# An earlier load of the next batch, and the last batch's masks, sums and row blocks placed otherwise, in a two-layer graph kernel

## The chip, the cores and the metric

The kernel runs on one core of one Trainium2 chip. The metric is the device time of the program in microseconds; three runs of the kernel before gave 4035.16, 4039.82 and 4045.39 us, the median is 4039.82 us. The profile that is quoted was taken from an execution of its own, with a span of 4048.5 us from the first to the last instruction.

Names in the profile: PE is TensorE's matmul, PEld its weight load, DVE is VectorE, ACT is ScalarE, POOL is GpSimd, SP is SyncE, whose queue (SPq) issues the transfers. L390 is line 390 of the kernel.

## The reference

Thirty-two independent batches `x[b]` of 512 nodes by 512 features go through two layers on one graph `adj` (512x512, zeros and ones), all in float32:

```python
# layer 0
deg = a.sum(axis=1)
out = deg[None, :, None] * (x @ Wi.T + b0) + einsum('ij,bjo->bio', a, x @ Wj.T)
x = layernorm(x + out)
# layer 1: attention with 8 heads of 64, masked by the graph
q, k, v = split_heads(x @ Wq.T + bq), split_heads(x @ Wk.T + bk), split_heads(x @ Wv.T + bv)
scores = where(adj == 0, -inf, q @ k.T / 8)
x = layernorm(x + (softmax(scores) @ v).reshape(...) @ Wo.T + bo)
```

## The kernel before

The program is one long sequence without a loop, with a schedule written by hand. Three batches are in work at once: while batch `b = n - 1` is in its attention (one "period" of eight steps), the products of batch `n` (layer 0, then Q, K, V), the start of batch `n + 1` and the output product of batch `n - 2` are placed between the steps as "pieces". A piece is a part of a 512x512x512 product by a seven-product scheme, with weights from a ring of twelve tiles that the sync queue fills. `z(...)` marks work that TensorE does not do.

Three buffers `xh` hold x, which is also where the result grows. So the load of batch `n + 1` needs the buffer whose last use is the store of batch `n - 2`:

```python
def load_x(b):
    XT[b] = work([P, NC, D], "xh", 3)
    nc.sync.dma_start(XT[b], rows(x[b]))
def store(b):
    nc.sync.dma_start(rows(out[b]), XT.pop(b))

def split(b, dc):            # x in two parts, for a product by adjR in a faster format
    ...
    nc.scalar.copy(hi, xs)                      # L183
    nc.gpsimd.tensor_sub(lo, xs, hi.bitcast(FT))  # L184
def ahead(b):
    split(b, 0)
    split(b, 1)

def l0_gather(b, dc, bank, adjT=None):
    ...
    for jc in range(NC):
        nc.tensor.transpose(pt[...], xt[:, jc, ...], ident)   # L292
    nc.vector.tensor_mul(XD[b][:, dc, :], pt, deg_r)          # L293
    ...
    nc.tensor.matmul(pm, parts[w][:, jc, :], adjR[:, jc, :], ...)  # L299, hi then lo
    nc.scalar.copy(AX_T[b][:, dc, :], pm)                     # L305
```

The part of a period in which Q, K and V are made, `ORDER` being `(1, 2, 6, 7, 4, 5, 3)`:

```python
    if m >= 0:
        res += [z(apply, m, 0), z(apply, m, 1), z(store, m)]
    for i in ORDER[2:]:
        for f in pc("q", n, i, K), pc("v", n, i, A):
            res += [f] + [g for g in side[:1] if g]
            side = side[1:]
        if i == 5 and n + 1 < B:
            res += [z(load_x, n + 1)] if n > 0 else []
    if n + 1 < B:
        res += [z(ahead, n + 1)]
    return res
```

Behind it comes `phase_a(n + 1)`, which begins with the four gathers of batch `n + 1`.

A step of the attention takes half the keys of a pair of heads. Blocks `kc` 0 and 1 belong to `half` 0, blocks 2 and 3 to `half` 1:

```python
def scores(b, hp, kc):
    ps = sc_tile()                                  # in PSUM, two of them
    for s in range(2): nc.tensor.matmul(ps[:, s, :], KT..., QT...)            # L427
    e = E[kc] = work([P, 2, N], "e", 4)
    nc.scalar.activation(ps, ps, AF.Exp, scale=QSCALE)                       # L431
    nc.vector.tensor_tensor(e, ps, edge[:, kc:kc+1, :].to_broadcast(...), op=OP.mult)  # L432
def presum(hp, half):
    if half == 0:
        ES[hp] = work([P, 2, N], "es", 1)
        nc.gpsimd.tensor_add(ES[hp], E[0], E[1])                             # L438
    else:
        nc.vector.tensor_add(ES[hp], ES[hp], E[half])                        # L440
def values(b, hp, half): ...   # PV[hp] += V.T @ E[kc]                         L448
def sums(b, hp): ...           # denominators: ones.T @ ES[hp]                 L455
def invert(b, hp, part): ...   # reciprocal of one block of 128 denominators   L461
def scale(b, hp): ...          # OT = PV * reciprocal, all 512 columns         L471
def tell(b, hp): ...           # sums up PV and reciprocal for a flag          L466
```

`PV` and the denominators share two PSUM buffers (`ov_tile`). In the last period only the output product of batch 30 (seven pieces), the bias adds of batch 31 (L326) and the first part of batch 31's own output product (`last_part`, L659) are left to place. Then comes the end:

```python
values(B - 1, HP - 1, 1)
sums(B - 1, HP - 1)
for hp in range(HP - 1):
    last_part(hp, 1)
for g in rest(B - 1, HP - 1):        # four inverts, scale
    if g[0] is not tell:
        g[0](*g[1:])
for ic in range(2):
    last_part(HP - 1, ic)
tell(B - 1, HP - 1)
for ic in range(NC):
    last_rows(ic)                    # add, statistics, normalise, store of 128 rows   L664
flags()
```

Of the kernel before, what the change touches and what calls it, by code (L numbers as in the profile page):

```python
# [17 lines left out]
P = 128  # L18
# [7 lines left out]
def gnn_attention_kernel(  # L26
# [51 lines left out]
    def work(shape, name, bufs, dtype=FT):  # L78
        return pools.work.tile(shape, dtype, name=name, bufs=bufs)
# [343 lines left out]
    def scores(b, hp, kc):  # L423
        ps = sc_tile()
        for s in range(2):
            r = slice(s * HD, (s + 1) * HD)
            nc.tensor.matmul(ps[:, s, :], KT[b, hp // 2][r, hp % 2, kc * P:(kc + 1) * P],  # L427
                             QT[b, hp // 2][r, hp % 2, :], start=True, stop=True)
        e = E[kc] = work([P, 2, N], "e", 4)

        nc.scalar.activation(ps, ps, AF.Exp, scale=QSCALE)  # L431
        nc.vector.tensor_tensor(e, ps, edge[:, kc:kc + 1, :].to_broadcast([P, 2, N]), op=OP.mult)  # L432

    def presum(hp, half):

        if half == 0:
            ES[hp] = work([P, 2, N], "es", 1)
            nc.gpsimd.tensor_add(ES[hp], E[0], E[1])  # L438
        else:
            nc.vector.tensor_add(ES[hp], ES[hp], E[half])  # L440

    def values(b, hp, half):
        if half == 0:
            PV[hp] = ov_tile()
        for kc in range(2 * half, 2 * half + 2):
            for s in range(2):
                c0 = hp * P + s * HD
                nc.tensor.matmul(PV[hp][s * HD:(s + 1) * HD, :], V[b][:, kc, c0:c0 + HD], E[kc][:, s, :],  # L448
                                 start=(kc == 0), stop=(kc == NC - 1))

    def sums(b, hp):

        pl = ov_tile()
        for s in range(2):
            nc.tensor.matmul(pl[s * HD:(s + 1) * HD, :], ones[:, :HD], ES[hp][:, s, :], start=True, stop=True)  # L455
        RL[hp] = (pl, work([P, N], "rl", 1))

    def invert(b, hp, part):
        pl, rl = RL[hp]
        c = slice(part * P, (part + 1) * P)  # L460
        nc.vector.reciprocal(rl[:, c], pl[:, c])  # L461
# [3 lines left out]
        j = b * HP + hp  # L465
        nc.vector.tensor_tensor_reduce(pl, pl, rl, 1.0, 0.0, OP.add, OP.add, told[:, j:j + 1])  # L466

    def scale(b, hp):
        if hp % 2 == 0:
            OT[b, hp // 2] = work([P, 2, N], "oT", 3)  # L470
        nc.vector.tensor_mul(OT[b, hp // 2][:, hp % 2, :], PV[hp], RL[hp][1])  # L471

    def rest(b, hp):
        return [(invert, b, hp, c) for c in range(4)] + [(scale, b, hp), (tell, b, hp)]
# [9 lines left out]
    def z(f, *a):  # L484
        return (0.0, f, *a)

    def pc(kind, b, i, bank):
        return (2 * PC if kind == "l0" else PC, piece, kind, b, i, bank)
# [62 lines left out]
    def phase_b(n):  # L551

        m = n - 2
        if m < 0:
            res = []
            side = [z(add_bo, 0, i) for i in range(2)]
            A, K = banks(n)
            for i, bank in ((2, A), (6, K), (5, A), (7, K), (3, A), (4, K)):
                res.append(pc("l0", n, i, bank))
                if i == 4:  # L560
                    res += [z(stats, n, 0)]
                res += side[:1]
                side = side[1:]
            return res + [z(apply, n, 0), z(stats, n, 1), (TR, l0_norm, n, 0), (TR, l0_norm, n, 1)]
        res = project(m, 1)
        for i in ORDER[1:]:
            res.append(pc("l0", n, i, banks(n)[0]))
            if i == 4:
                res.append(z(stats, n, 0))
            if i == 5:  # L570
                res.append(z(stats, m, 0))
            if i == 3:
                res += [z(stats, n, 1), (TR, l0_norm, n, 1)]
            res += project(m, i)
            if i == 4:
                res.append(z(apply, n, 0))
            if i == 5:
                res.append((TR, l0_norm, n, 0))
            if i in (7, 4):
                res.append(z(add_bo, n - 1, int(i == 4)))  # L580
        return res

    def phase_c(n):

        m = n - 2
        norm = [(TR, l0_norm, n, ic) for ic in range(NC)]
        h = lambda j, i: quarter(HT[n], j, i)
        A, K = banks(n)
        res = [pc("v", n, 1, A)] + ([z(apply, n, 1)] if n else []) + [pc("q", n, 1, K)]
        if m >= 0:  # L590
            res += [z(stats, m, 1)]
        res += [pc("v", n, 2, A), norm[2], norm[3], z(combos, TH, n, h, (1, 2)), pc("k", n, 1, A),
                z(combos, TH, n, h, (3, 4)), pc("q", n, 2, K), pc("k", n, 2, A)]
        side = []
        if n == 0:

            side = [z(graph_forms, 2), None, z(graph_forms, 0), None, z(graph_forms, 1)]
# [3 lines that stand above are left out]
            for f in pc("q", n, i, K), pc("v", n, i, A):  # L601
                res += [f] + [g for g in side[:1] if g]
                side = side[1:]
            if i == 5 and n + 1 < B:
                res += [z(load_x, n + 1)] if n > 0 else []
        if n + 1 < B:
            res += [z(ahead, n + 1)]
        return res

    def fold(part):  # L610
# [21 lines left out]
    def last_steps():  # L632

        m = B - 2
        p = [pc("pj", m, i, bank) for i, bank in ALONE]
        c = [z(combos, TO, m, ot_quarter(m), (1, 2)), z(combos, TO, m, ot_quarter(m), (3, 4))]
        own = [(4 * GA, last_part, hp, 0) for hp in range(3)]
        return [[z(last_load), p[0], FLUSH] + c + [z(add_bo, B - 1, 0), z(add_bo, B - 1, 1)], [p[1], p[2]], [p[3], p[4]], [p[5], p[6], z(stats, m, 0), z(stats, m, 1)],
                [FLUSH, own[0], z(apply, m, 0), z(apply, m, 1), z(store, m)], [own[1]], [FLUSH, own[2]], []]

    def run(f):
        f[1](*f[2:])
# [5 lines left out]
        t = load_w(work([P, NC, D], "xh", 3), woT, nc.sync)  # L648
        W["wo"] = [t[:, 0:2, :], t[:, 2:4, :]]

    def last_part(hp, half):
        if hp == 0:
            if half == 0:
                ACC[0], ACC[1] = mm_tile("a"), mm_tile("b")
            else:
                t = sc_tile()
                ACC[2], ACC[3] = t[:, 0, :], t[:, 1, :]
        for ic in range(2 * half, 2 * half + 2):
            nc.tensor.matmul(ACC[ic], OT[B - 1, hp // 2][:, hp % 2, ic * P:(ic + 1) * P], W["wo"][hp // 2][:, hp % 2, :],  # L659
                             start=(hp == 0), stop=(hp == HP - 1))  # L660

    def last_rows(ic):
        y = XT[B - 1][:, ic, :]
        nc.vector.tensor_add(y, y, ACC[ic])  # L664
        MV["last", ic] = work([P, 5], "mv", 12)
        ln_stats(MV["last", ic], y)
        ln_apply(MV["last", ic], y)
        nc.sync.dma_start(rows(out[B - 1])[:, ic, :], y)
# [23 lines left out]
    for n in range(1, B + 1):  # L692
        b = n - 1
        extra = []
        for step in range(STEPS):
            hp, half = divmod(step, 2)
            scores(b, hp, 2 * half)
            scores(b, hp, 2 * half + 1)
            if step > 0:
                ph, phalf = divmod(step - 1, 2)  # L700
                values(b, ph, phalf)
                if phalf == 1:
                    sums(b, ph)
                    extra = rest(b, ph)
            elif b > 0:
                values(b - 1, HP - 1, 1)
                sums(b - 1, HP - 1)
                extra = rest(b - 1, HP - 1)
            late = [(presum, hp, 0)] if half == 0 else [(presum, hp, 2), (presum, hp, 3)]
            for f in PERIODS[n][step]:  # L710
                if f is FLUSH:
                    some = len(extra)
                else:
                    run(f)

                    some = 0 if f[0] == 0.0 else len(extra) if step == 0 else max(1, round(f[0] / PC))
                if some:
                    for g in late[:1] + extra[:some]:
                        g[0](*g[1:])
                    late, extra = late[1:], extra[some:]  # L720
            for g in late + extra:
                g[0](*g[1:])
            extra = []
    values(B - 1, HP - 1, 1)
    sums(B - 1, HP - 1)
    for hp in range(HP - 1):
        last_part(hp, 1)
    for g in rest(B - 1, HP - 1):
        if g[0] is not tell:
            g[0](*g[1:])  # L730
    for ic in range(2):
        last_part(HP - 1, ic)
    tell(B - 1, HP - 1)
    for ic in range(NC):
        last_rows(ic)
    flags()
    fast.close()
    flag = nc.values_load(again[0:1, 0:1], min_val=0, max_val=1)
# [134 lines left out]
```

## Time and profile before

| | |
|---|---|
| median of three runs | 4039.82 us (4035.16 to 4045.39) |
| span of the profile, mean granted TensorE clock | 4048.5 us, 0.986 |
| DMA, mean over the span | 107 GB/s |
| one load of x, 1 MB, issue to landing (median) | 5.7 us |
| one store of a batch, 1 MB, issue to landing (median) | 5.2 us |
| mask on VectorE, 128x1024 (L432), mean of 512 | 1218 ns |
| sum of two blocks on GpSimd (L438), mean of 128 | 2349 ns |
| from one batch's store to the next (1043.6 to 1168.6 us) | 125.0 us |
| last period, first scores to last normalised row | 3949.1 to 4042.5 us |

How to read what is quoted below: in a list of waits, each line names who waited, for whom, the idle time in us, how often and the longest. In a timeline, a line begins with start and duration in us, then engine, line, operation and tiles (out<-in), and the count if several like ones were merged; brackets hold the engine's idle time before it and what ended it. Matmuls are pipelined and their ends are modelled, so durations of neighbours overlap a little. The granted clock is a share of TensorE's full speed.

### The profile page before, as it was taken

The page shows a single profiled execution, that of the slowest core. Times are in us where ns is not written, and L with a number is a line of the kernel's source. Part 1 is how long each engine was busy: PE and PEld are TensorE (multiplying, and loading weights), DVE is VectorE, ACT ScalarE, POOL GpSimd, SP SyncE. Part 2 cuts the span into 40 slices and gives each one's busy share as a digit, 9 for nine tenths or more (in the row PEclk, how much of TensorE's full clock was granted, in tenths as well). Part 3 has the DMA queues.
Part 4 walks back from the last instruction along what each step waited for, and adds up shares of the span by engine and source line. Part 5 has one row for each costly group of instructions (what it writes and reads, how often), then busy time and mean ns, then how long its engine had stood idle before and what let it go on. Part 6 is the DMA issues. An engine that isn't in the chain of part 4 may idle for free.

```text
span 4048.5 us, 46895 instructions
## 1 busy us (share of the span) xinstructions
PE 3902.1 (96%) x17370; PEld 2663.9 (66%) x17370; DVE 2595.3 (64%) x3525; ACT 1058.3 (26%) x1476; POOL 1862.8 (46%) x1861
## 2 busy tenths in 40 slices
PE   9999999999999999999999999999999999999997
PEld 6666666666666666666666666666666666666663
DVE  4566665666666666666666666666666666666666
ACT  2222222222222222222223222222222222222322
POOL 4355444454434544345444445443454434544433
PEclk9999999999999999999999999999999999999998
DMA  7333333333334233333333433333423333333330
GB/s 247 107 104 97 110 99 115 107 98 104 110 106 123 84 112 102 108 117 92 104 110 104 117 105 100 103 107 110 122 81 111 106 110 114 104 97 110 102 110 22
DMA packets 281866, 433.86 MB, mean 107 GB/s; under 512 B 23073, under 2 KB 119841, under 8 KB 281633
## 3 DMA queue, kind: packets, MB, share of 16 engines
q1 hardware_dynamic: 281376, 430.27, 35.3%
q8 instruction: 141, 2.31, 0.2%
q14 instruction: 93, 0.75, 0.1%
q0 software_dynamic: 256, 0.53, 0.0%
HBM read 389.29 MB, written 41.42 MB: 106 GB/s over the span
## 4 chain that ended last, share of the span: by engine, by line
PE 72%; DVE 11%; POOL 9%; DMA 4%; issue 2%; ACT 1%; SPq 0%; POOLq 0%
PE mma L375 20%; PE mmb L375 20%; PE sc L427 10%; PE ov L448 9%; POOL xh L390 5%; DMA xh<-in_x_dram 4%; PE mmb L299 3%; PE mma L299 3%; DVE rl L461 3%; PE ov L455 2%; DVE st L265 2%; DVE xh L393 2%; POOL big L344 2%; DVE e L432 2%; POOL es L438 2%
## 5 line engine op out<-in xcount | busy, mean ns | idle before, releaser
L432 DVE TENSOR_TENSOR e<-sc,edge 128x1024 f32<-128x1024 f32 x512 | 602.4, 1218 | 467.3 <-ACT sc L431 467.3
L431 ACT ACTIVATE sc<-sc 128x1024 f32<-128x1024 f32 x512 | 492.9, 1007 | 1279.8 <-PE sc L427 1279.3
L375 PE MATMUL mmb<-ring,big 128*128 128x256 f32 x3144 | 734.6, 382 | 7.9 <-POOL big L344 7.9
L375 PE MATMUL mma<-ring,big 128*128 128x256 f32 x3112 | 724.2, 381 | 3.1 <-POOL big L344 2.9
L375 PEld LDWEIGHTS mmb<-ring,big 128*128 128x128 f32 x3144 | 593.2, 191 | 131.4 <-DVE e L432 23.5
L375 PEld LDWEIGHTS mma<-ring,big 128*128 128x128 f32 x3112 | 584.7, 190 | 125.4 <-DVE e L432 25.2
L344 POOL TENSOR_TENSOR big<-big 128x512 f32<-128x512 f32 x376 | 549.7, 1488 | 222.3 <-DVE big L293 177.9
L184 POOL TENSOR_TENSOR xlo<-xh,xhi 128x512 fp32r<-128x512 f32 x128 | 163.4, 1287 | 911.6 <-ACT xhi L183 909.4
L427 PE MATMUL sc<-q,k 64*128 64x512 f32 x2048 | 513.8, 620 | 0.0
L448 PE MATMUL ov<-e,v 128*64 128x512 f32 x2048 | 497.8, 607 | 8.2 <-DVE oT L471 8.2
L461 DVE RECIPROCAL rl<-ov 128x128 f32<-128x128 f32 x512 | 462.4, 929 | 5.6 <-PE ov L455 1.8
L375 PE MATMUL mma<-big,ring 128*128 128x256 f32 x1808 | 433.1, 382 | 2.2 <-DVE xh L393 2.2
L375 PE MATMUL mmb<-big,ring 128*128 128x256 f32 x1776 | 425.3, 382 | 3.2 <-DVE xh L393 2.4
L267 POOL TENSOR_SCALAR mv<-mv 128x1 f32<-128x1 f32 x256 | 50.3, 196 | 747.2 <-DVE mv L266 737.1
L375 PEld LDWEIGHTS mma<-big,ring 128*128 128x128 f32 x1808 | 337.9, 190 | 80.5 <-issue 26.0
L375 PEld LDWEIGHTS mmb<-big,ring 128*128 128x128 f32 x1776 | 332.2, 190 | 78.7 <-issue 24.3
L438 POOL TENSOR_TENSOR es<-e 128x1024 f32<-128x1024 f32 x128 | 300.7, 2349 | 176.5 <-PE ov L455 176.5
L448 PEld LDWEIGHTS ov<-e,v 128*64 128x64 f32 x2048 | 124.8, 136 | 349.0 <-issue 275.3
L440 DVE TENSOR_TENSOR es<-es,e 128x1024 f32<-128x1024 f32 x256 | 339.6, 1327 | 0.1
L427 PEld LDWEIGHTS sc<-q,k 64*128 64x128 f32 x2048 | 178.8, 189 | 214.4 <-issue 212.2
L393 DVE TENSOR_TENSOR xh<-xh,mmb 128x512 f32<-128x512 f32 x186 | 125.7, 676 | 217.4 <-PE mmb L375 216.4
L390 POOL TENSOR_TENSOR xh<-xh,p 128x512 f32<-128x512 f32 x186 | 231.7, 1274 | 72.4 <-ACT sc L431 39.0
(141 smaller groups left out, 3746.1 us busy)
## 6 DMA issues: line engine op xcount, KB each, us to landing
ring<-wq SPq DMA_DIRECT2D x160, 256.0 KB, 2.6
ring<-wv SPq DMA_DIRECT2D x160, 256.0 KB, 2.7
ring<-wk SPq DMA_DIRECT2D x160, 256.0 KB, 3.8
ring<-wi SPq DMA_DIRECT2D x155, 256.0 KB, 2.7
ring<-wj SPq DMA_DIRECT2D x155, 256.0 KB, 2.7
ring<-wo SPq DMA_DIRECT2D x155, 256.0 KB, 2.6
xh<-in_x_dram SPq DMA_DIRECT2D x32, 1024.0 KB, 5.7
out_dram<-xh SPq DMA_DIRECT2D x31, 1024.0 KB, 5.2
```

The source lines that it names most:

```text
L299: nc.tensor.matmul(pm, parts[w][:, jc, :], adjR[:, jc, :], start=(w == 0 and jc == 0), stop=(w == 1 and jc == NC - 1))
L344: nc.gpsimd.tensor_tensor(dst, p, q, op=OP.subtract)
L375: nc.tensor.matmul(pm[:, c * Q:(c + 1) * Q], lhs, rhs, start=first, stop=(kc == 1 and n == len(terms) - 1), skip_group_check=True)
L390: nc.gpsimd.tensor_tensor(d, d, p1, op=OP.add)
L393: nc.vector.tensor_tensor(d, d, pm, op=OP.add)
L427: nc.tensor.matmul(ps[:, s, :], KT[b, hp // 2][r, hp % 2, kc * P:(kc + 1) * P], QT[b, hp // 2][r, hp % 2, :], start=True, stop=True)
L431: nc.scalar.activation(ps, ps, AF.Exp, scale=QSCALE)
L432: nc.vector.tensor_tensor(e, ps, edge[:, kc:kc + 1, :].to_broadcast([P, 2, N]), op=OP.mult)
L438: nc.gpsimd.tensor_add(ES[hp], E[0], E[1])
L440: nc.vector.tensor_add(ES[hp], ES[hp], E[half])
L448: nc.tensor.matmul(PV[hp][s * HD:(s + 1) * HD, :], V[b][:, kc, c0:c0 + HD], E[kc][:, s, :], start=(kc == 0), stop=(kc == NC - 1))
L461: nc.vector.reciprocal(rl[:, c], pl[:, c])
```

## The change

The load of the next x moves up in the sync queue, closer behind the store that frees its buffer, and the splitting of x moves up too; the aim is that x is there when the gathers of the next batch begin. In the second batch, two pieces of layer 0 change places. In the last batch, where TensorE has less to do, GpSimd masks one block of each step (all but the very last) and sums one block per pair of heads; ScalarE then writes the exponentials of those blocks to SBUF. The last denominators are accumulated by TensorE from all four blocks, without a sum ahead, and the end inverts, scales, multiplies and finishes row block by row block. The output pieces of batch 30 are placed in another order.

```diff
@@ scores
         e = E[kc] = work([P, 2, N], "e", 4)
+        if b == B - 1 and (kc == 1 or kc == 3 and hp < HP - 1):
+            nc.scalar.activation(e, ps, AF.Exp, scale=QSCALE)
+            nc.gpsimd.tensor_tensor(e, e, edge[:, kc:kc + 1, :].to_broadcast([P, 2, N]), op=OP.mult)
+            return
@@ presum
-            nc.vector.tensor_add(ES[hp], ES[hp], E[half])
+            (eng or nc.vector).tensor_add(ES[hp], ES[hp], E[half])
+    def end_of(b, hp):
+        pl = ov_tile()
+        RL[hp] = (pl, work([P, N], "rl", 1))
+        for kc in range(NC):
+            for s in range(2):
+                r, c0 = slice(s * HD, (s + 1) * HD), hp * P + s * HD
+                if kc >= 2:
+                    nc.tensor.matmul(PV[hp][r, :], V[b][:, kc, c0:c0 + HD], E[kc][:, s, :], start=False, stop=(kc == NC - 1))
+            for s in range(2):
+                nc.tensor.matmul(pl[s * HD:(s + 1) * HD, :], ones[:, :HD], E[kc][:, s, :], start=(kc == 0), stop=(kc == NC - 1))
@@ phase_b, second batch
-            for i, bank in ((2, A), (6, K), (5, A), (7, K), (3, A), (4, K)):
+            for i, bank in ((2, A), (6, K), (5, A), (7, K), (4, K), (3, A)):
@@ phase_c
+            if i == 7 and 0 < n < B - 1:
+                res += [z(load_x, n + 1)]
             if i == 5 and n + 1 < B:
-                res += [z(load_x, n + 1)] if n > 0 else []
-        if n + 1 < B:
-            res += [z(ahead, n + 1)]
+                res += [z(ahead, n + 1)]
@@ last_steps: output pieces of batch 30, by number
-        steps: [1] [6, 2] [7, 5] [4, 3]          (shortened)
+        steps: [1] [2, 6] [5, 7] [3, 4]          (shortened)
@@ the last period's sums
+            if b == B - 1:
+                late = [] if hp == HP - 1 else [(presum, hp, 0, nc.gpsimd)] if half == 0 else [late[0], late[1] + (nc.gpsimd,)]
@@ the end
-    values(B - 1, HP - 1, 1)
-    sums(B - 1, HP - 1)
+    end_of(B - 1, HP - 1)
     for hp in range(HP - 1):
         last_part(hp, 1)
-    ... (inverts, scale, last_part(HP - 1, 0 and 1))
+    for ic in range(NC):
+        invert(B - 1, HP - 1, ic)
+        scale(B - 1, HP - 1, slice(ic * P, (ic + 1) * P))
+        last_part(HP - 1, ic=ic)
+        if ic > 0:
+            last_rows(ic - 1)
     tell(B - 1, HP - 1)
-    for ic in range(NC):
-        last_rows(ic)
+    last_rows(NC - 1)
```

`scale` and `last_part` gain a parameter each for one block of 128.

More of the change, by code (lines that the diff above doesn't have):

```diff
@@ L429, in scores, with presum @@
         e = E[kc] = work([P, 2, N], "e", 4)
+        if b == B - 1 and (kc == 1 or kc == 3 and hp < HP - 1):
+            nc.scalar.activation(e, ps, AF.Exp, scale=QSCALE)
+            nc.gpsimd.tensor_tensor(e, e, edge[:, kc:kc + 1, :].to_broadcast([P, 2, N]), op=OP.mult)
+            return
         nc.scalar.activation(ps, ps, AF.Exp, scale=QSCALE)
         nc.vector.tensor_tensor(e, ps, edge[:, kc:kc + 1, :].to_broadcast([P, 2, N]), op=OP.mult)
-    def presum(hp, half):
+    def presum(hp, half, eng=None):
         if half == 0:
@@ L466, in tell, with scale @@
         nc.vector.tensor_tensor_reduce(pl, pl, rl, 1.0, 0.0, OP.add, OP.add, told[:, j:j + 1])
-    def scale(b, hp):
+    def scale(b, hp, c=slice(0, N)):
         if hp % 2 == 0:
             OT[b, hp // 2] = work([P, 2, N], "oT", 3)
-        nc.vector.tensor_mul(OT[b, hp // 2][:, hp % 2, :], PV[hp], RL[hp][1])
+        nc.vector.tensor_mul(OT[b, hp // 2][:, hp % 2, c], PV[hp][:, c], RL[hp][1][:, c])
     def rest(b, hp):
@@ L634, in last_steps @@
         m = B - 2
-        p = [pc("pj", m, i, bank) for i, bank in ALONE]
+        p = {i: pc("pj", m, i, bank) for i, bank in ALONE}
         c = [z(combos, TO, m, ot_quarter(m), (1, 2)), z(combos, TO, m, ot_quarter(m), (3, 4))]
         own = [(4 * GA, last_part, hp, 0) for hp in range(3)]
-        return [[z(last_load), p[0], FLUSH] + c + [z(add_bo, B - 1, 0), z(add_bo, B - 1, 1)], [p[1], p[2]], [p[3], p[4]], [p[5], p[6], z(stats, m, 0), z(stats, m, 1)],
-                [FLUSH, own[0], z(apply, m, 0), z(apply, m, 1), z(store, m)], [own[1]], [FLUSH, own[2]], []]
+        return [[z(last_load), p[1], FLUSH] + c + [z(add_bo, B - 1, 0), z(add_bo, B - 1, 1)], [p[2], p[6]], [p[5], p[7]],
+                [p[3], p[4], z(stats, m, 0), z(stats, m, 1)], [FLUSH, own[0], z(apply, m, 0), z(apply, m, 1), z(store, m)],
+                [own[1]], [FLUSH, own[2]], []]
     def run(f):
@@ L649, in last_load, with last_part @@
         W["wo"] = [t[:, 0:2, :], t[:, 2:4, :]]
-    def last_part(hp, half):
+    def last_part(hp, half=None, ic=None):
         if hp == 0:
@@ L657, in last_part @@
                 ACC[2], ACC[3] = t[:, 0, :], t[:, 1, :]
-        for ic in range(2 * half, 2 * half + 2):
+        for ic in (range(2 * half, 2 * half + 2) if ic is None else (ic,)):
             nc.tensor.matmul(ACC[ic], OT[B - 1, hp // 2][:, hp % 2, ic * P:(ic + 1) * P], W["wo"][hp // 2][:, hp % 2, :],
@@ L723, in gnn_attention_kernel @@
             extra = []
-    values(B - 1, HP - 1, 1)
-    sums(B - 1, HP - 1)
+    end_of(B - 1, HP - 1)
     for hp in range(HP - 1):
         last_part(hp, 1)
[L728 to L732, printed above, removed]
+    for ic in range(NC):
[4 more added lines that the diff above has]
+            last_rows(ic - 1)
     tell(B - 1, HP - 1)
-    for ic in range(NC):
-        last_rows(ic)
+    last_rows(NC - 1)
     flags()
```

## The prediction

> **What bounds the kernel now.** I read first the page's busy shares, then the table of waits for TensorE alone, then one batch in the timeline where the longest wait falls, then the last batch.
>
> ```profile
> PE 3902.1 (96%) x17370; PEld 2663.9 (66%) x17370; DVE 2595.3 (64%) x3525; ACT 1058.3 (26%) x1476; POOL 1862.8 (46%) x1861
> PE sc L292 <- DMA xh<-in_x_dram: 89.3, 30, 5.5
> PE ov L448 <- DVE oT L471: 8.2, 4, 3.0
> PE mmb L375 <- POOL big L344: 7.9, 15, 5.0
> ```
>
> TensorE is busy 96% of the span and idle for 4048.5 - 3902.1 = 146 us. Of these, 89.3 us have one cause: thirty times, once in each of batches 2 to 31, the transposes that open the layer-0 gather (L292) wait for the transfer of x. No other wait passes 9 us in total. So this wait is what can be had in the body of the kernel. What it costs is more than the idle time, as the timeline of one batch shows (start, duration, engine, line; the bracket is the idle time before and its releaser):
>
> ```profile
> 1043.61 0.39 SPq L477 DMA_DIRECT2D out_dram<-xh  x1
> 1058.19 0.42 SPq L107 DMA_DIRECT2D xh<-in_x_dram  x1
> 1059.26 1.89 PE L375 MATMUL mma<-ring,big 128*128 128x256 f32 x8
> 1063.94 0.66 PE L292 MATMUL sc<-ident,xh 128*128 128x128 f32 x4 [2.79 <-DMA xh<-in_x_dram]
> 1064.59 1.41 PE L299 MATMUL mmb<-adjR,xhi 128*128 128x512 f32 x4
> 1065.96 2.08 PE L299 MATMUL mmb<-adjR,xlo 128*128 128x512 f32 x4
> 1067.96 2.39 PE L427 MATMUL sc<-q,k 64*128 64x512 f32 x8
> ...
> 1074.84 0.60 PE L292 MATMUL sc<-ident,xh 128*128 128x128 f32 x4
> 1075.19 1.17 PE L299 MATMUL mmb<-adjR,xhi 128*128 128x512 f32 x4
> 1076.20 1.08 PE L299 MATMUL mmb<-adjR,xlo 128*128 128x512 f32 x4
> 1077.12 1.89 PE L375 MATMUL mma<-big,ring 128*128 128x256 f32 x8
> 1061.15:1067.96 6.81, 4.02 (x12) 2.25 (x12) 1.38 (x2) 1.14 (x2) 2.52 (x2) 0.81 0.50 187
> 1074.84:1077.12 2.28, 2.28 (x13) 1.94 (x12) 2.08 (x4) 0.00 (x0) 0.68 (x1) 1.00 0.41 104
> ```
>
> The last two lines are the window view of the same stretches: after the window's length, busy time of PE, weight load, DVE, ACT, POOL, then granted clock, DMA share and GB/s. The first gather of the batch takes 6.81 us from the end of the last V piece (1059.26 + 1.89 = 1061.15) to the next scores; the second, which is the same work with its data there, takes 2.28 us. The difference, 4.5 us, is 2.8 us of waiting, 0.6 us until GpSimd has the low part, and slow matmuls: the four xlo products take 2.08 us against 1.08, at a granted clock of 0.81 against 1.00.
>
> **What the Trainium skill says.** "TensorE: Matmul & The Clock Gate", section "HAM oscillation — how this bites in real kernels": a wait for DMA that lasts about one activity window sends TensorE back to half its clock, and the work behind pays again. The trace agrees: 2.08 us for what takes 1.08 us elsewhere. "DMA: Bandwidth & Descriptors", section "Anatomy of one DMA — SWDGE (gpsimd) path": a semaphore wait is served on the issuing sequencer before dispatch. The trace shows the sync queue standing at its store until ScalarE is done (163.8 us in 31 times); so a load moved up stands in the queue until its buffer is free, and the weight loads behind it stand too. "GPSIMD Engine Reference", section "3.1 Elementwise — side-by-side cycle accounting": a two-input operation costs GpSimd 1.96 times what it costs VectorE. Here the add of 128x1024 takes 2349 ns on GpSimd (L438) and 1218 ns median on VectorE (L440), 1.93 times. The section "8. Key points" of that page says that GpSimd cannot reach PSUM; the trace has nothing against it, and it is why the masked blocks of the change get their exponentials in SBUF.
>
> **The change, part by part.**
>
> Load of x. In the queue the load stood behind the fifth pair of q/v pieces and now stands behind the q/v pair 7, four pieces and one step of scores and values earlier. In the batch shown that pair's weight prefetch issues at 1046.9. The load needs the buffer that the store issued at 1043.61 is reading; stores land a median 5.2 us after issue, so it leaves at about 1048.8 instead of 1058.19, and at the median 5.7 us lands at about 1054.5. TensorE wants it at 1061.15: 6.6 us to spare, more than the longest wait of the table (5.5). The copies and subtractions that split x (L183, L184) move ahead by one pair of pieces and then find x there; ScalarE's next work behind them is the gather's own copy (1068.07) and the exponentials (1069.54), and GpSimd has nothing from 1043 to 1061, so they push nothing. The weight ring holds twelve tiles, some 20 us of pieces at about 1.73 us from start to start, so a pause of 2 us in the queue is covered. Over all thirty first gathers the time from the preceding matmul to the next work that is not gather adds up to 203.6 us, 6.79 us each; undisturbed they would take 30 x 2.28 = 68.4. **Gain: 135 us.** In eleven batches the scores behind the gather also ran slow, 2.04 to 2.51 us for 1.99, together 3.4 us. **Sum: 139 us.**
>
> Order of the second batch's last two layer-0 pieces (4 before 3). Before, TensorE waited 2.86 us at 143.58 for the first normalised rows and ran the next 2 us slowly; its next piece began at 145.76 instead of about 141.9, and took 0.7 us too long. Piece 4 now follows piece 7 in the same bank and waits about 0.9 us for VectorE to read it. **Gain: 3.7 us.**
>
> Last batch. It goes from the scores at 3949.1 to the end and is not bound by TensorE (72.0 us busy of 93.5).
>
> ```profile
> 3967.42 6.92 POOL L326 TENSOR_TENSOR xh<-xh,bo_r 128x512 f32<-128x512 f32 x4
> 3973.13 1.94 PE L448 MATMUL ov<-e,v 128*64 128x512 f32 x8
> 4024.27 2.47 DVE L440 TENSOR_TENSOR es<-es,e 128x1024 f32<-128x1024 f32 x2
> 4026.89 1.08 PE L455 MATMUL ov<-es,ones 128*64 128x512 f32 x4 [1.27 <-DVE es L440]
> 4027.90 5.42 PE L659 MATMUL sc<-xh,oT 128*128 128x512 f32 x12
> 4034.22 0.69 DVE L664 TENSOR_TENSOR xh<-xh,mma 128x512 f32<-128x512 f32 x1 [1.43 <-PE mma L659]
> ```
>
> It takes 7 masks (1218 ns) and 3 sums (1218 ns) from VectorE, 12.2 us, and puts 10 x 2.35 = 23.5 us on GpSimd; the last head pair's three sums go altogether. Where it helps: piece 2 fills 1.9 of the 5.0 us in which TensorE waits for the differences of the attention output, and the next scores come 2 to 4 us earlier. Where it hurts: GpSimd works in order. Its second mask stands behind the bias adds, which end at 3974.3, so it ends at 3976.7, and the sum behind it at 3979.0; the value products that wait for that mask ran at 3973.13 before, and the denominators at 3974.9. I take 5 us lost there. VectorE's shorter queue gives some of it back where reciprocals come late (4.1 us between the denominators' end at 3995.5 and the next values at 4002.40, 2.98 of it idle TensorE): I keep 3 us lost at the last scores.
>
> The end. Before, from the values at 4021.97: sums on VectorE to 4026.74, denominators to 4027.97. Now TensorE does 1.94 us of values, then eight products with ones and four more values, 6 pairs x 0.97 = 5.8 us, ending at 4029.7: 1.8 us later. Then 5.42 us of output products come first in both versions. Before, all four reciprocals and the scaling (4.1 us) and the flag sum (0.8 us) lay in their shadow. Now two row blocks' reciprocals and scalings do; the other two (0.95 + 0.25 us each) stand between the rows of the first blocks, as does the flag sum: 2.4 + 0.8 = 3.2 us more on VectorE, which ends the kernel. **Last batch: 3 + 1.8 + 3.2 = 8 us lost.**
>
> Sum: 4039.8 - 139 - 3.7 + 8 = **3905 us**.
>
> **The rivals.** (1) *The wait moves to the store.* If the store came later than in the batch shown, or store and load hindered each other, part of the wait would stay. For it: 1 MB takes 5.2 us, at 244 GB/s with the weight loads in that window, and one batch had a gap of 5.5 us. Against it: 6.6 us to spare. With half of the cost left: 3975 us. (2) *Another engine takes over.* VectorE is at 64% and GpSimd at 46%; against 125 us per batch minus 4.6 they rise by 4% of themselves. No TensorE wait on either passes 9 us in total, so I give it little; 1 us a batch would make 3935 us. (3) *The idle time is gone but the clock pays.* If TensorE were granted less clock when it no longer rests, each per cent would cost 39 us. Against it: in the stretches with no gap the windows show 1.00 over 43 us. (4) *The last batch is the better half.* If GpSimd's queue is not the hindrance that I make of it, these 8 us fall to about 0 or -5: 3892 to 3897 us.
>
> **Range and chances.** The terms of the sum that can move are the last batch (8, give or take 8), what is left of the first gather (0 to 10 us) and the three runs' own scatter (4035 to 4045). I say 3905 us, 3888 to 3922 eight times in ten. Faster by over 2% means under 3959; half of the load's gain lost would miss it, and nothing seen points there: 0.97 faster, 0.025 same, 0.005 slower.
>
> **What would show it.** Right: no DMA wait before L292 from batch 2 on, the first gather at about 2.3 us, a store-to-store distance of about 120.5 us instead of 125.0, the load issued some 5 us behind the store. For the last batch: value products waiting for a GpSimd mask in its second step, VectorE idle before the first final rows, and from its first scores to the last normalised row about 8 us more than before. Wrong: a wait on the new load, or weight tiles arriving late because the queue stood, or the time of the first gather going to a wait on VectorE.

## The result, and the profile after

The changed kernel takes 3918.7 us, median of four runs (3917.13 to 3919.22); four runs of the kernel before gave 4041.39 us (4035.16 to 4045.39). The ratio is 0.9697 (95% interval 0.968 to 0.9714): 3.0% faster. The prediction said 3905 us, 3888 to 3922.

Busy shares, from the page of the changed kernel:

```profile
PE 3856.6 (98%) x17382; PEld 2642.6 (67%) x17382; DVE 2595.7 (66%) x3516; ACT 1058.0 (27%) x1476; POOL 1920.0 (49%) x1870
```

TensorE's idle time fell from 146 to 3915.4 - 3856.6 = 59 us, and its busy time from 3902.1 to 3856.6 us although it has 12 instructions more. Of these 45.5 us, 41.6 lie in the thirty first gathers (115.0 us busy before, 73.4 now), where the same matmuls ran at a higher clock; the mean granted clock rose from 0.986 to 0.996. The head of TensorE's list of waits:

```profile
PE mmb L375 <- POOL big L344: 6.9, 15, 4.0
PE ov L453 <- DVE oT L488: 6.1, 4, 2.5
PE sc L160 <- DVE big L154: 6.0, 3, 4.2
```

The wait for x (89.3 us before) is not shortened, it is gone, and behind the prologue no other wait of TensorE on a transfer has come in its place. The same part of a batch in the timeline; it is the batch after the one quoted before (10 instead of 9), so the products go to the other bank, `mma`:

```profile
1126.62 0.39 SPq L494 DMA_DIRECT2D out_dram<-xh  x1
1131.91 0.37 SPq L107 DMA_DIRECT2D xh<-in_x_dram  x1
1137.49 1.14 ACT L183 CAST xhi<-xh 128x512 fp32r<-128x512 f32 x2 [2.92 <-DMA xh<-in_x_dram]
1137.89 1.22 DVE L445 TENSOR_TENSOR es<-es,e 128x1024 f32<-128x1024 f32 x1
1138.18 4.27 POOL L184 TENSOR_TENSOR xlo<-xh,xhi 128x512 fp32r<-128x512 f32 x2 [14.76 <-ACT xhi L183]
1143.99 0.60 PE L292 MATMUL sc<-ident,xh 128*128 128x128 f32 x4
1144.35 1.18 PE L299 MATMUL mma<-adjR,xhi 128*128 128x512 f32 x4
1145.37 1.07 PE L299 MATMUL mma<-adjR,xlo 128*128 128x512 f32 x4
```

The load leaves 5.3 us behind the store, as soon as its buffer is free; the sync queue stands for that buffer 41.6 us in 29 times, and TensorE does not notice. x is there at 1137.49, 6.5 us before TensorE's transposes at 1143.99 ask for it (predicted 6.6; over the thirty batches x lands 4.9 to 8.6 us before the first gather). No bracket stands before those. The window view of that first gather (length, busy time of PE, PEld, DVE, ACT, POOL, then clock, DMA share, GB/s) shows no rest and the full clock, for the 6.81 us and 0.81 of before:

```profile
1143.99:1146.37 2.38, 2.38 (x13) 1.76 (x11) 1.29 (x2) 0.00 (x0) 0.00 (x0) 1.00 0.66 195
```

All thirty first gathers, measured as in the prediction from the preceding matmul's end, take 66.3 us together (203.6 before). From store to store a batch takes 120.06 us (mean of the 28 between 285.78 and 3647.58; 124.64 before).

### The profile page after: what moved, and what is told of

It reads as the page before. It is cut to its first block, busy times and chain, and to the rows that moved or that the text cites. A ratio compares the mean times of both kernels' runs of the same rounds, so it can differ in the third digit from the quotient of the medians.

```text
span 3915.4 us, 46926 instructions
## 1 busy us (share of the span) xinstructions
PE 3856.6 (98%) x17382; PEld 2642.6 (67%) x17382; DVE 2595.7 (66%) x3516; ACT 1058.0 (27%) x1476; POOL 1920.0 (49%) x1870
## 5 line engine op out<-in xcount | busy, mean ns | idle before, releaser
L184 POOL TENSOR_TENSOR xlo<-xh,xhi 128x512 fp32r<-128x512 f32 x128 | 202.0, 1588 | 737.7 <-ACT xhi L183 737.7
L445 DVE TENSOR_TENSOR es<-es,e 128x1024 f32<-128x1024 f32 x251 | 349.2, 1391 | 1.4 <-POOL es L443 1.3
L393 DVE TENSOR_TENSOR xh<-xh,mma 128x512 f32<-128x512 f32 x186 | 125.8, 676 | 223.4 <-PE mma L375 223.4
```

Of the source, the lines that this page charges most:

```text
L393: nc.vector.tensor_tensor(d, d, pm, op=OP.add)
L445: (eng or nc.vector).tensor_add(ES[hp], ES[hp], E[half])
```

## The experiments

The offsets given for the last batch are read in each run's timeline, from the first scores of the last period.

### The load alone, the last batch alone, both without the last batch

**Load alone**: the kernel before with the two lines of `phase_c` from the change's diff and nothing else.

> The kernel before with nothing but the load of x and its splitting moved up. Theory (the wait on x is nearly all of the gain, the last batch costs): all first gathers at 2.2 us, no DMA wait at L292, and about 3912 us: the change's 3918.7 less 10.5 for its last batch, plus 3.7 for the second batch's order. Rival (the last batch of the change brings part of the gain): slower than the change, 3925 us or more.

Measured: 3911.74 us (3909.25 to 3913.35); ratio to before 0.9664 (0.9648 to 0.968). The first gathers add up to 66.3 us.

**Last batch alone**: the change with these lines put back:

```diff
-            if i == 7 and 0 < n < B - 1:
-                res += [z(load_x, n + 1)]
-            if i == 5 and n + 1 < B:
-                res += [z(ahead, n + 1)]
+            if i == 5 and n + 1 < B:
+                res += [z(load_x, n + 1)] if n > 0 else []
+        if n + 1 < B:
+            res += [z(ahead, n + 1)]
```

> The whole change with the load and the splitting put back where they were. Theory: the last batch costs about 10 us and the second batch's order gains 3.7, so this is 5 to 8 us slower than the kernel before, and the DMA waits are all there. Rival (the last batch is the better half): some us faster than the kernel before.

Measured: 4053.72 us, median of 20 (4043.93 to 4067.92), against 4049.01 for 31 runs of before; ratio 1.0015 (1.0006 to 1.0024), which is 2 to 10 us more. The waits for x are all there (89.3 us in 30 times).

**Load and order**: the load alone, and the second batch's pieces as in the change, `(7, K), (4, K), (3, A)`.

> The change with its last batch put back: load and splitting moved up, and the second batch's two pieces changed over. Theory: about 3908 us, 10 us under the change and 3.7 under the load alone. Rival (the last batch pays): 3919 or more.

Measured: 3908.06 us (3907.21 to 3909.08); ratio 0.9655 (0.9639 to 0.9671). So the load's move is the whole gain and more. The order of two pieces is worth 3.7 us, as worked out: the last matmul before batch 2's first gather ends at 183.66 us here and at 187.44 us with the load alone. Eleven traces with the new order have it at 182.7 to 184.4, the three with the old one at 187.4 to 187.9. The last batch of the change costs 3918.7 - 3908.06 = 10.6 us.

### The kernel before, a second time

> The kernel before once more, for a second trace. The runs of before scatter over 10 us, those of the change over 2 us, and the trace of before that the prediction was read from belongs to an execution of 4050 us, 9 to 10 us above the median. Theory: what scatters is the wait on x itself, so this trace's time and its sum of first gathers move together: per us that the span is shorter than 4048.5, about 1 us less in the thirty first gathers (203.6 us there). Rival: the scatter lies elsewhere, and the first gathers add up to 203 us again whatever the span.

Measured: this trace's execution took 4054.12 us, its span is 4052.3 us. TensorE's first wait, and that of the last batch alone in the second fence:

```profile
PE sc L292 <- DMA xh<-in_x_dram: 93.6, 30, 4.7
```

```profile
PE sc L292 <- DMA xh<-in_x_dram: 89.3, 30, 4.9
```

Between the first gathers of batches 2 and 31, three traces with the late load give 3608.79, 3614.02 and 3620.30 us, with 199.2, 203.6 and 208.0 us in the first gathers: time and gathers go together, 4.4 us of gathers to 5.2 and 6.3 us of time. With the load behind pair 7 that stretch takes 3480.9 to 3481.9 us in each of nine traces. The runs say the same: the standard deviation is 4.9 us over 31 runs of before and 6.0 over 20 of the last batch alone, but 1.7 and 0.9 over four runs each of the load alone and of load and order. So much of the scatter sits in the first gathers.

It is not the wait alone that scatters. The traces with 199.2 us (the last batch alone) and 203.6 us (before) wait equally long for x, 89.3 us; they differ in how often the slow clock follows. The mean granted clock over the 5 us from the transposes on is below 0.75 in 17 of the thirty gathers in the first and in 22 in the second, and 1.00 in the others. Up to 3.4 us the length of the wait on x does not decide it: in the trace of before a wait of 2.29 us was followed by 0.68, one of 2.92 us by 1.00. In these traces every wait on x over 3.4 us was followed by the slow clock. No trace of one of the shortest executions of before (4035 to 4040 us) is at hand; that they spend some 10 us less in the first gathers is inferred.

### How early the load must be

Both on load and order. **Behind pair 4** (`if i == 4` for `if i == 7`):

> As the run with load and order changed, but the load stands behind pair 4 of the q/v pieces, one step later than in the change and one pair earlier than before. By the change's trace it would issue at about 1137.7 in the batch quoted, land 5.7 us later at 1143.4, and TensorE asks for it at 1143.96. Theory (only the landing time counts): hardly any spare time, so 0 to 1 us per batch is lost, 3909 to 3935 us, with the waits in the batches whose transfer takes longest. Rival (how close the load stands to the store matters in itself): most of the old cost stays, 3975 us or more.

Measured: 3913.49 us (3909.37 to 3917.15). TensorE's list has 1.1 us on x in two times, and the first gathers add up to 74.4 us, 8.1 more than with the load at pair 7. The landing time decides, not nearness to the store. The load issues a median 6.4 us ahead of the first gather, against 3.0 in the kernel before and 12.3 in the change: 3.4 of the 9.3 us by which the change moves it do for all but some 5 us, and the rest is spare time against late transfers.

**Behind pair 3**, the splitting behind it:

```diff
-            if i == 7 and 0 < n < B - 1:
+            if i == 3 and 0 < n < B - 1:
                 res += [z(load_x, n + 1)]
-            if i == 5 and n + 1 < B:
-                res += [z(ahead, n + 1)]
+        if n + 1 < B:
+            res += [z(ahead, n + 1)]
```

> As the run with load and order changed, but the load stands behind the last pair, 3.5 us later than in the kernel before, with the splitting behind it. Theory: each first gather waits 3.5 us longer than before and runs somewhat colder, so 30 x 3.5 to 30 x 4.5 us more than before: 4135 to 4170 us. Rival (the wait is filled by other work, or the cost was the clock alone): 4060 us or less.

Measured: 4144.69 us, ratio to before 1.0243 (1.0218 to 1.0268). One first gather in its timeline:

```profile
1080.59 0.39 SPq L107 DMA_DIRECT2D xh<-in_x_dram  x1
1085.99 1.12 PE L292 MATMUL sc<-ident,xh 128*128 128x128 f32 x4 [5.87 <-DMA xh<-in_x_dram]
1086.76 2.06 PE L299 MATMUL mmb<-adjR,xhi 128*128 128x512 f32 x4
1088.61 1.19 PE L299 MATMUL mmb<-adjR,xlo 128*128 128x512 f32 x4
```

The wait is 5.87 us here, 178.6 us in all (89.3 before), and the transposes and the first products behind it run at about half speed (1.12 and 2.06 us for 0.60 and 1.18). The thirty gathers add up to 304.2 us, 237.9 more than at pair 7, and the time is 4144.69 - 3908.06 = 236.6 us more. What a late x costs is the gather's lengthening, wait and slow clock together.

**Load early, splitting where it was:**

> As the run with load and order changed, but the splitting of x stays at the end of the phase, where it was. Theory: ScalarE and GpSimd have nothing else queued in that stretch, so the splitting starts when x lands or its two pieces are passed in any case, and the time is the same within 2 us. Rival: the earlier splitting is a part of the gain, some 0.6 us a batch for the low part and a slow clock behind it, 20 to 40 us slower.

Measured: 3906.99 us (3905.86 to 3909.0). The splitting's move does nothing for the time: with x there, ScalarE comes to it early enough by itself.

### The last batch in parts

Each on load and order (3908.06 us, last normalised row at 93.08 us from the last period's first scores; the whole change has it at 103.54). The runs come from several chips; three kernels that are nearly the same (load and order, the splitting left where it was, and the piece order below) took 3908.06, 3906.99 and 3907.89 us on three of them, so the chip counts for little here.

**GpSimd's masks and sums alone** (`scores` and `presum` as in the change, the last pair keeps its sums):

> Load and order changed, and of the last batch's changes only the masks and sums on GpSimd (the last pair of heads keeps its sums, the last two of them on VectorE; end and output pieces as before). Theory: GpSimd's second mask stands behind the bias adds and TensorE waits for it, so it is 3 to 8 us slower than without. Rival: VectorE is the bound there and the time falls by a few us.

Measured: 3908.6 us (3907.33 to 3910.97), last row at 94.59 us. The loss is less than expected, though TensorE does wait for GpSimd (1.52 and 1.35 us, quoted below), and the rival's gain is not there either.

**The end alone** (`end_of`, and row block by row block):

> Load and order changed, and of the last batch's changes only the end: denominators from all four blocks and the end row block by row block (the last pair has no sums). Theory: 4 to 7 us slower than without, as the last two reciprocals and the flag sum stand between the rows on VectorE and TensorE, waiting between row blocks, falls to a slower clock. Rival: the end is the part that gains, and it is some us faster.

Measured: 3913.76 us (3910.62 to 3915.45), last row at 98.47 us: 5.7 us slower, as expected.

**The order of the output pieces alone:**

> Load and order changed, and of the last batch's changes only the order of the output pieces of batch 30. Theory: piece 2 fills a part of the wait for the differences, so it is 1 to 3 us faster. Rival: the time is made up at the next wait, and nothing changes.

Measured: 3907.89 us (3904.56 to 3909.78), last row at 93.11 us. The third step's scores come 1.3 us earlier (20.56 for 21.85), and the last scores later (70.0 for 69.4): the rival's case.

**Masks, sums and piece order together, the old end:**

> Load and order changed, and of the last batch's changes the masks and sums on GpSimd together with the order of the output pieces; end as before. Apart, the two cost 0.5 and -0.2 us and the end 5.7 us, 6.0 in sum, while all three together cost 10.6. Theory (they add up badly: with piece 2 ahead the scores come earlier and TensorE waits longer for the same GpSimd mask, so its clock drops): 3912 to 3914 us, with a granted clock under 0.8 in the last batch's third step. Rival (the missing 4 us belong to the end, or to chance in where the clock drops): 3907 to 3910 us.

Measured: 3913.64 us (3909.49 to 3915.53), last row at 97.48 us, and the scores of every step within 0.2 us of where the whole change has them. Two changes of half a microsecond or less make 5.6 together, and with the end's 5.7 they account for the 10.6. The granted clock in the third step is 0.78; with GpSimd's part alone it is 1.00. The third step without the new piece order (the run with GpSimd's part alone), then with it:

```profile
3832.28 1.08 PE L453 MATMUL ov<-e,v 128*64 128x512 f32 x4 [1.52 <-POOL e L433]
3834.70 1.08 PE L460 MATMUL ov<-es,ones 128*64 128x512 f32 x4 [1.35 <-POOL es L445]
3835.71 1.99 PE L375 MATMUL mmb<-ring,big 128*128 128x256 f32 x8
```

```profile
3832.12 1.08 PE L453 MATMUL ov<-e,v 128*64 128x512 f32 x4 [2.86 <-POOL e L433]
3834.55 1.98 PE L460 MATMUL ov<-es,ones 128*64 128x512 f32 x4 [1.34 <-POOL es L445]
3836.45 3.75 PE L375 MATMUL mma<-ring,big 128*128 128x256 f32 x8
```

GpSimd's mask ends where its queue lets it: it releases TensorE 26.3 to 26.4 us after the period's first scores in all four traces that have it. TensorE, there sooner, waits 2.86 us instead of 1.52, and then runs the next products at half speed: 1.98 us for 1.08, and 3.75 for 1.99. In these executions the earlier arrival is paid twice. It need not be. The last batch alone has the same masks and piece order; in its trace the clock was slow one step earlier (the third step's scores took 3.11 us for 1.99), TensorE came late to the mask, waited 1.59 us and kept 1.08 and 1.99 us behind it. And waits of up to 3.4 us on x were followed now by the slow clock, now by the full one. So the longer wait and the slow products are shown; that this order always costs 5 us is not, and the four runs, 6 us apart, may well hold both cases.

### A version that follows from this

Load and order, the output pieces in the new order, masks and sums on VectorE as before, and:

```diff
-                [own[1]], [FLUSH, own[2]], []]
+                [own[1]], [FLUSH], [own[2]]]
@@ the last denominators: ones times (blocks 0 + 1), 2 and 3
+        blocks = [ES[hp], E[2], E[3]]
@@ the end: four inverts, scale, two products, tell, then the rows (as before the change)
```

> Load and order changed, output pieces in the new order, masks and sums on VectorE as before; the output product of the third pair of heads is put behind the last scores instead of ahead of them, where TensorE waited 4.2 us for VectorE; the last denominators from the sum of blocks 0 and 1 and from blocks 2 and 3 (three products, not four), all reciprocals ahead of the rows. Theory: 6 to 9 us faster than load and order alone, about 3900 us. Rival: the last rows are bound by VectorE alone and only 1 or 2 us are gained.

Measured: 3903.36 us (3899.51 to 3905.54); ratio to before 0.9651 (0.9635 to 0.9667), against 0.9697 (0.968 to 0.9714) for the change. It is 4.7 us faster than load and order, short of the 6 to 9 expected. Last row at 88.65 us, 4.4 us before that of load and order. The last scores came 8 us earlier (61.4 for 69.4), but half of that was given back, as its timeline shows:

```profile
3867.66 1.99 PE L427 MATMUL sc<-q,k 64*128 64x512 f32 x8
3867.78 3.39 DVE L474 RECIPROCAL rl<-ov 128x128 f32<-128x128 f32 x4 [0.19 <-PE ov L455]
3872.04 1.94 PE L448 MATMUL ov<-e,v 128*64 128x512 f32 x8 [2.39 <-DVE oT L484]
3873.91 1.12 PE L673 MATMUL mma<-xh,oT 128*128 128x512 f32 x2
3879.31 1.03 PE L469 MATMUL ov<-e,ones 128*64 128x512 f32 x4
```

TensorE still waits for the third pair's scaling, which frees the buffer of the last values, and then has 8 us of products in a row.

## Why the prediction was right, and where it was off

**The load of x: right.** "Sum: 139 us" stood on a trace of 4048.5 us. The thirty first gathers lost 203.6 - 66.3 = 137.3 us against 135, and none of the scores behind them runs slow; before, they did so in twelve batches for 3.8 us together, not in eleven for 3.4. The span fell by 4048.5 - 3915.4 = 133.1 us against 139 + 3.7 - 8 = 134.7. Removing the wait and the slow clock behind it as one cost was the step that carried the result; the idle time alone, 89.3 us, would have given two thirds.

**The order of two pieces: right**, 3.7 us predicted, 3.7 measured. TensorE's wait of 2.86 us for the normalised rows is gone, and one of 0.8 us on VectorE stands in its place, where 0.9 was expected.

**The last batch: right in kind, 8 predicted, 10.6 measured.** The masks behind the bias adds, the two waits on GpSimd and the rows behind reciprocals are there. Lines of the changed kernel's timeline:

```profile
3824.43 4.94 POOL L326 TENSOR_TENSOR xh<-xh,bo_r 128x512 f32<-128x512 f32 x4
3829.33 2.12 POOL L433 TENSOR_TENSOR e<-e,edge 128x1024 f32<-128x1024 f32 x1
3831.50 1.08 PE L453 MATMUL ov<-e,v 128*64 128x512 f32 x4 [2.86 <-POOL e L433]
3835.83 3.78 PE L375 MATMUL mma<-ring,big 128*128 128x256 f32 x8
...
3898.17 1.13 PE L677 MATMUL sc<-xh,oT 128*128 128x512 f32 x2 [2.03 <-DVE oT L488]
3900.88 1.98 PE L677 MATMUL sc<-xh,oT 128*128 128x512 f32 x2 [1.58 <-DVE oT L488]
3902.89 0.69 DVE L682 TENSOR_TENSOR xh<-xh,sc 128x512 f32<-128x512 f32 x1 [2.07 <-PE sc L677]
```

Against the trace of before, the last scores are 4.7 us later, where I had kept 3, the denominators 5.0 against 4.8, the last row 10.1 against 8. The mis-sized terms are "I keep 3 us lost at the last scores" and "3.2 us more on VectorE": the latter measured 5.1. It left out that TensorE, resting between row blocks, takes 1.98 us for two products that take 1.02 elsewhere, and that VectorE waits 2.07 us for them. The 3 us rest in part on a wrong reading: from 3995.5 to 4002.40 are 6.9 us, and 4.1 us is what the reciprocals and the scaling take in that time. I also treated the piece order as a gain of 1.9 us that adds to the rest; in this trace it turned a cheap wait into a dear one. How much depends on the execution: in the trace of the last batch alone the last row is 5.7 us later than before, not 10.1.

**The starting point: the step that was off most.** "4039.8 - 139 - 3.7 + 8" takes the terms of one execution from the median of others. The trace belonged to an execution of 4050.38 us, 10.6 us above that median. Subtracted from its own time, the same terms give 4050.4 - 134.7 = 3915.7 us, against 3917.13 for the profiled execution of the change. Of the 13.7 us between 3905 and 3918.7, this is 10.6. Two chances add up in it: over all 68 runs of before the median is 4046.6 us, so the traced execution was 3.8 us slow, and the three runs behind 4039.82 were 6.8 us fast. The range held, with 3 us to spare, because it allowed for the scatter of the three runs and for 8 us either way in the last batch.

## What to carry to other kernels

When a load waits at the head of a dense stretch, count the stretch's lengthening against an undisturbed copy of itself, not the idle time. Then see how much spare time the transfer has; more than its own scatter is enough. A saving read from a trace comes off that execution's time, above all where the thing removed is itself what scatters; and three runs are few where they scatter over 10 us. Where TensorE is no longer the bound, reaching a wait sooner can cost time by the clock behind it, so measure such parts together and not only apart.

## What the runs showed of the hardware that I had not expected

- GpSimd's subtraction in the split (L184, 128x512) slows down beside one kind of VectorE work. Alone it takes 1.26 to 1.29 us, and beside VectorE's masks, which read PSUM, 1.26 to 1.27; beside VectorE's sums of two tiles in SBUF (L445 after the change) up to 2.26. Where two of them met such sums, from 1137.89 on, they took 4.27 us together, against 2.52 when they ran in the gap of before; the mean rose from 1287 to 1588 ns, at no cost to the time.
- GpSimd's mask, float32 times bfloat16 into the same tile, takes 2.125 us for 128x1024 (median of 7), less than its sum of two float32 blocks (2.35).
- The same instructions take different times according to when the clock drops. The third step of the last period took 15.9 us in the changed kernel and 12.8 us in the last batch alone. Windows of the first, then of the second (from 0.07 us after its scores began):

```profile
3825.40:3841.30 15.90, 11.70 (x37) 5.85 (x36) 3.47 (x4) 1.94 (x2) 12.81 (x8) 0.77 0.00 0
```

```profile
3957.60:3970.30 12.70, 9.76 (x36) 4.67 (x36) 3.47 (x4) 2.03 (x2) 12.38 (x7) 0.91 0.00 0
```

The same operations of VectorE and ScalarE are in both; only the granted clock (0.77 and 0.91) and with it TensorE's busy time and waits differ.
